# The node stage of a graph layer made in two passes: source rows first, target rows second

## The chip, the cores and the metric

One core of one Trainium2 chip runs the kernel. The metric is the device time of one execution in microseconds (us). The engines are TensorE (PE; PEld is its weight loads), VectorE (DVE), ScalarE (ACT), GpSimd (POOL) and SyncE (SP), and 16 DMA engines move data.

## The reference

The layer has N = 12500 nodes with C = 128 channels and E = 400000 edges, sorted by target. A node's row is normalised and clipped, and every edge makes a message from its source's and its target's row; attention weights over the edges of a target sum the messages up.

```python
h = jnp.maximum(_layernorm(x), 0.0)
msg_src = h @ w_src + b_src
msg_dst = h @ w_dst
message = (msg_src[src] + msg_dst[dst]) * edge_weight * radial_mlp(edge_attr)
message = message @ w_sep + b_sep            # 8 heads of 16 alpha and 16 value channels
alpha, value = smooth_leaky_relu(message[:, :, :16]), message[:, :, 16:]
score = einsum(alpha, alpha_dot)             # one number per edge and head
att = segment_softmax(score, dst)
out = segment_sum(value * att, dst) @ w_proj + b_proj
return x + out
```

The radial MLP has two hidden layers of 64 with silu, on 32 edge attributes.

## The kernel before, in words

The kernel has a node stage, an edge stage and a tail, all written with an order fixed by hand: each engine executes its instructions in the order of the program text, and semaphores, placed by the framework, make one engine wait for another.

**Node stage (lines 150 to 347, 0 to about 111 us).** The 12500 rows are 98 tiles of up to 128 rows, in 25 groups of four ("quads"). x is loaded whole into `x_all` at the start. `stats` (L214) takes mean and variance of a group of tiles on DVE (L218, L219), the square root on ACT (L221), the reciprocal and the shift on DVE (L222, L223). `norm(i)` (L231) makes h = relu(x * rstd + shift) of a quad on ACT, four instructions. `turn(i)` transposes the four tiles on PE (L240), and DVE copies the turned quad from PSUM to `hT` (L243). `products(i)` multiplies each tile by w_src and w_dst side by side, 256 columns (L255, PE), copies the result from PSUM to `ms` on ACT (L261) or for some on DVE (L259), and SP stores it to two DRAM tables, `t_src` and `t_dst` (L266, L268). The loop over the quads issues, for quad i: `stats` of two quads where i is even, `norm(i+2)`, `turn(i+1)`, `products(i)`. Besides, SP issues `load_targets` at i = 5 (all 400000 targets into `cur`, and the ends of all sections of 500 edges) and `load_weights` at i = 9 (33 small loads); at i = 15 `fits` counts on DVE whether the targets are sorted (L273 a comparison, L276 a sum) and every section spans less than 64 rows (`bad`, which chooses between this path and a slower one that these inputs don't take); at i = 20 `cuts` marks on DVE where the target changes (L305, `sm`), and makes small constants with PE and DVE (`bvb`, L313, `pv`, `pb`).

**Edge stage (`windows`, L663; about 111 to 4115 us).** It works in steps of 1000 edges, two sections of 500; `step(k)` runs for k from -5 to 399 and holds one piece each of several steps, later ones ahead of earlier ones. The pieces that matter here:

- `prep_load(u)`, `prep_make(u)`, `prep_turn(u)` (L675 to L706): for 16 steps, the source numbers of the edges are loaded by SP, turned by PE into a list `idx` for the gathers, and the targets into `loc`. For u = 0 they stand ahead of the first step, later ones inside steps.
- `load_e` (L710, issued by ACT), `load_w`, `load_md`, `load_d`, `load_sm` (issued by SP): edge attributes `e_t`, edge weights `w_b`, the 64 rows of t_dst from the section's first target on (`md`, L727, at an address read from `base`), the targets, and the marks.
- `zero(i)` (L131, SP): the output table `agg` is set to zero in 20 stores from `z`, two a step in steps 0 to 9.
- `gather(k, f)` (L749, POOL): for each 128 edges one indirect DMA brings the 128 source rows of t_src into `gs0` or `gs1`, of three buffers each. 3125 of them in all, 7.8 a step. In step k stand the gathers of step k+2.
- `e_T`, `mlp1`, `mlp2`, `mlp3`, `radial`: the radial MLP.
- `sources(k, f)` (L819, L822, PE) turns the gathered rows into PSUM; `message(k)` (L829) adds the target rows there by a product with the one-hot matrix `ohT`, and multiplies by the radial part (L835, `mT`, DVE).
- `alphas`, `scores` (L840 to L864) and, 13 steps later (`LAG`), `values` and `sums` (L926, L937).

**Tail (about 4115 to 4313 us).** Window sums are combined, and the finish stage makes the output projection (L1304, `py`) and adds x.

The functions that the change touches, with the lines of the profile:

Of the kernel before, what the change touches and what calls it, by code (L numbers as in the profile page):

```python
# [30 lines left out]
P = 128  # L31
# [25 lines left out]
def gnn_kernel(ctx: ExitStack, tc: tile.TileContext, a: dict, out: bass.AP):  # L57
# [68 lines left out]
    dst_h = dst.rearrange("(k f e) -> f k e", f=2, e=SEC)  # L126
# [22 lines left out]
    with tc.tile_pool(name="node", bufs=2) as np_, tc.tile_pool(name="node1", bufs=1) as n1, \  # L149
# [15 lines left out]
        CC = E // P  # L165
        cur = n1.tile([P, CC + 1], I32, name="cur")
# [9 lines left out]
        def load_targets():  # L176

            nc.sync.dma_start(out=cur[:, 1:CC + 1], in_=dst.rearrange("(p c) -> p c", p=P))
            at = dst[CC - 1:CC]
            with nc.allow_non_contiguous_dma(reason="single targets"):  # L180
                nc.sync.dma_start(out=cur[1:P, 0:1], in_=bass.AP(at.tensor, at.offset, [[CC, P - 1], [1, 1]]))
                for f in range(2):
                    nc.sync.dma_start(out=base[:, f, :], in_=dst_h[f:f + 1, :, 0])
                at = dst[0:1]
                nc.sync.dma_start(out=ends, in_=bass.AP(
                    at.tensor, at.offset, [[8 * SEC, 100], [SEC, 8], [SEC - 1, 2]]))

        def load_weights():
            for name, t in wt.items():
                ap = a[name]  # L190
                if name == "b_src":
                    ap = ap.rearrange("o c -> c o")
                elif name == "b_proj":
                    ap = ap.to_broadcast([P, C])
                nc.sync.dma_start(out=t, in_=ap)
            for f in range(2):
                for q in range(2):
                    o = (2 * q + f) * RAD
                    nc.sync.dma_start(out=w1b[o:o + RAD, f * FC:(f + 1) * FC], in_=a["fc_w1"])
                s = slice(f * FC, (f + 1) * FC)  # L200
                for q in range(2):
                    nc.sync.dma_start(out=w2b[s, q * FC:(q + 1) * FC], in_=a["fc_w2"])
                nc.sync.dma_start(out=w3b[s, :], in_=a["fc_w3"])
                nc.sync.dma_start(out=b12[s, 0:1], in_=a["fc_b1"])
                nc.sync.dma_start(out=b12[s, 1:2], in_=a["fc_b2"])
# [6 lines left out]
        hs, hTs = {}, {}  # L212
        G = 8
        def stats(t0, t1):  # L214
            for t in range(t0, t1):
                n = rows(t)
                st = np_.tile([P, nc.vector.BN_STATS_DIM], F32, name="st", bufs=4)
                nc.vector.bn_stats(st[:n], x_all[:n, t, :])  # L218
                nc.vector.bn_aggr(mv[:n, t, :], st[:n])  # L219
            s = slice(t0, t1)  # L220
            nc.scalar.activation(rstd[:, s], mv[:, s, 1], AF.Sqrt, bias=eps, scale=1.0)  # L221
            nc.vector.reciprocal(rstd[:, s], rstd[:, s])  # L222
            nc.vector.scalar_tensor_tensor(shift[:, s], mv[:, s, 0], -1.0, rstd[:, s],  # L223
                                           op0=ALU.mult, op1=ALU.mult)
# [21 lines left out]
        def products(i):  # L246
            t0, t1 = quads[i]
            hT = hTs.pop(i)
            ms = np_.tile([P, 2, 4, C], F32, name="ms", bufs=6)
            for v0 in range(t0, t1, 2):  # L250
                vs = range(v0, min(v0 + 2, t1))
                pm = nps.tile([P, 2, 2, C], F32, name="pm", bufs=4)
                for t in vs:
                    n = rows(t)
                    nc.tensor.matmul(pm[:n, t - v0], hT[:, t - t0, :n], w_nodes, start=True, stop=True)  # L255
                for n, u0, u1 in blocks(v0, vs[-1] + 1):
                    o, q = ms[:n, :, u0 - t0:u1 - t0, :].rearrange("p k j c -> p j k c"), pm[:n, u0 - v0:u1 - v0]
                    if v0 % 16 == 2:
                        nc.vector.tensor_copy(o, q)  # L259
                    else:  # L260
                        nc.scalar.copy(o, q)  # L261
# [41 lines left out]
        def cuts():  # L303
# [16 lines left out]
            nc.vector.tensor_scalar(b_s, pb, 0.25, None, op0=ALU.mult)  # L320
            nc.vector.tensor_sub(far, eb[:, :, 1], eb[:, :, 0])
# [339 lines left out]
    def windows():  # L661
# [5 lines left out]
        with tc.tile_pool(name="wk2", bufs=2) as sp, tc.tile_pool(name="ps", bufs=1, space=PSUM) as pp, \  # L667
                tc.manual_schedule(), ExitStack() as held:
            lp = held.enter_context(tc.tile_pool(name="ld", bufs=2))
            prep, e_g, d_g, w_g, md, gath = {}, {}, {}, {}, {}, {}  # L670
            eTs, h1s, h2s, ohT, m3, mr, mTs, als, S_all, sms, Ps, Pem, pvx, ohs, accs, xs, Ms, pms, p3s, rads = (
                {} for _ in range(20))


            def prep_load(u):  # L675
# [10 lines left out]
                prep[u] = (ri, rb)  # L686

            def prep_make(u):
                ri, rb = prep[u]
# [5 lines left out]
                prep[u] = rows  # L695

            def prep_turn(u):
                rows = prep[u]
# [3 lines left out]
                idx = lp.tile([P, T], I32, name="idx")  # L702
                nc.vector.tensor_copy(idx, pt[:, 0, 0:T])
# [660 lines left out]
```

## Time and profile before

| quantity | value |
|---|---|
| median of 3 runs (lowest, highest) | 4316.28 us (4314.72, 4322.2) |
| the profiled execution | 4315.26 us |
| its span | 4313.4 us |
| mean granted clock of TensorE | 0.977 |
| first and last gather (L749) start | 118.41 and 4107.08 us |
| DMA over the span | 790.10 MB, 183 GB/s |

The page has the busy time of each engine, the span in 40 slices, the DMA queues, the chain of work that ended last, and the costliest groups of instructions. A line of the timeline reads: start, duration, engine, line, operation, tile written and tiles read, count, and in brackets the idle time of the engine before it with what ended that. A line of the waits reads: engine, tile and line that waited, what it waited for, total us, times, longest us.

### The profile page before, as it was taken

What the parts mean: (1) busy time and instruction counts of PE and PEld (TensorE: products, weight loads), DVE (VectorE), ACT (ScalarE), POOL (GpSimd) and SP (SyncE); (2) the same over time, 40 slices, a digit from 0 to 9 for tenths busy, and PEclk for the clock granted to TensorE, in tenths of its full rate; (3) what the DMA queues carried; (4) which work ended last, traced back from release to release, by engine and by line L of the source; (5) the groups of instructions that cost most, each with busy time, mean ns of one, the idle gap of its engine ahead of it and who ended that gap; (6) DMA issues with size and microseconds to landing.
All of it is one profiled execution on the core that took longest, in us unless ns stands there. A gap on an engine that the chain in (4) does not pass through costs nothing.

```text
span 4313.4 us, 91919 instructions
## 1 busy us (share of the span) xinstructions
PE 4065.7 (94%) x31567; PEld 2626.4 (61%) x31567; DVE 3101.8 (72%) x5980; ACT 2105.5 (49%) x4995; POOL 3037.4 (70%) x3148
## 2 busy tenths in 40 slices
PE   6679999999999999999999999999999999999974
PEld 5346666666666666666666666666666666666653
DVE  7357777777777777777777777777777777777776
ACT  6335555555455455455555455454555545544521
POOL 0667777777777777777777777777777777777701
PEclk8789999999999999999999999999999999999987
DMA  5667777777777777777777777777777767777725
GB/s 207 196 183 183 183 193 184 192 194 185 194 188 186 192 190 186 192 183 185 198 186 193 185 177 190 183 182 185 175 181 188 177 182 184 182 185 178 173 59 190
DMA packets 598603, 790.10 MB, mean 183 GB/s; under 512 B 125595, under 2 KB 475424, under 8 KB 597996
## 3 DMA queue, kind: packets, MB, share of 16 engines
q1 hardware_dynamic: 394314, 520.94, 43.1%
q0 software_dynamic: 100416, 205.45, 23.2%
q10 hardware_dynamic: 103394, 57.74, 5.1%
q8 instruction: 250, 4.10, 0.4%
q14 instruction: 229, 1.88, 0.1%
HBM read 643.48 MB, written 140.67 MB: 182 GB/s over the span
## 4 chain that ended last, share of the span: by engine, by line
PE 80%; DMA 8%; ACT 3%; DVE 3%; issue 2%; POOL 2%; SPq 1%; ACTq 0%; POOLq 0%; DVEq 0%
PE V L926 16%; PE pa L840 14%; PE misc L937 9%; PE pm L829 6%; PE p L800 6%; PE pm L819 6%; PE p L783 5%; PE m L768 5%; PE m L854 4%; PE pm L822 4%; DMA gs<-t_src,idx 4%; POOL gs L749 2%; PE m L759 2%; ACT L842 1%; DMA agg<-z 1%
## 5 line engine op out<-in xcount | busy, mean ns | idle before, releaser
L749 POOL DMA_INDIRECT gs<-t_src,idx x3125 | 3023.0, 967 | 1082.9 <-issue 778.6
L842 ACT ACTIVATE sl<-pa,c_b_a 128x500 f32<-128x500 f32 x800 | 541.8, 677 | 1004.4 <-PE pa L840 996.8
L926 PEld LDWEIGHTS V<-c_w_v,mT 128*125 128x125 f32 x6192 | 735.3, 188 | 479.8 <-DVE ohT L793 231.9
L928 DVE TENSOR_TENSOR pvx<-V,Pem 125x512 f32<-125x512 f32 x774 | 530.9, 686 | 524.2 <-PE V L926 495.5
L926 PE MATMUL V<-c_w_v,mT 128*125 128x128 f32 x6192 | 875.3, 285 | 0.2 <-DVE pvx L928 0.2
L840 PE MATMUL pa<-mT,c_w_a 128*128 128x500 f32 x1600 | 817.4, 593 | 53.8 <-DVE al L847 51.8
L847 DVE SCALAR_TENSOR_TENSOR al<-pa,sl 128x500 f32<-128x500 f32 x800 | 542.3, 678 | 239.6 <-ACT sl L842 227.0
L822 PEld LDWEIGHTS pm<-ident,gs 128*128 128x128 f32 x2350 | 418.6, 192 | 380.0 <-issue 359.5
L807 DVE SCALAR_TENSOR_TENSOR rad<-p,c_fc_b,w_b 128x500 f32<-128x500 f32 x800 | 553.3, 733 | 104.2 <-PE p L800 101.4
L835 DVE SCALAR_TENSOR_TENSOR mT<-pm,c_b_src,rad 128x500 f32<-128x500 f32 x800 | 553.2, 733 | 79.9 <-PE pm L829 66.1
L937 PE MATMUL misc<-pvx,oh 125*64 125x136 f32 x6400 | 463.7, 288 | 0.0
L937 PEld LDWEIGHTS misc<-pvx,oh 125*64 125x64 f32 x6400 | 361.1, 138 | 163.7 <-ACT eT L761 157.3
L819 PE MATMUL pm<-ident,gs 128*128 128x128 f32 (+9 forms) x2725 | 436.9, 275 | 13.1 <-DMA gs<-t_src,idx 12.7
L800 PE MATMUL p<-h,w3b 64*128 64x500 f32 x1600 | 406.5, 585 | 11.1 <-ACT h L786 11.1
L786 ACT ACTIVATE h<-p,b 128x500 f32<-128x500 f32 x400 | 326.3, 816 | 177.1 <-PE p L783 134.5
L941 ACT COPY ob<-misc 128x136 f32<-128x136 f32 x400 | 108.9, 272 | 618.3 <-PE misc L937 533.7
L822 PE MATMUL pm<-ident,gs 128*128 128x12 f32 (+30 forms) x2350 | 384.2, 244 | 16.5 <-DMA gs<-t_src,idx 15.7
L819 PEld LDWEIGHTS pm<-ident,gs 128*128 128x128 f32 (+9 forms) x2725 | 339.2, 157 | 30.2 <-DMA gs<-t_src,idx 18.3
L829 PE MATMUL pm<-ohT,m 64*128 64x500 bf16 x2400 | 325.6, 378 | 0.0
L840 PEld LDWEIGHTS pa<-mT,c_w_a 128*128 128x128 f32 x1600 | 243.1, 192 | 81.4 <-DVE al L847 65.6
L768 PE MATMUL m<-eT,w1b 64*128 64x250 f32 x800 | 276.7, 426 | 7.5 <-ACT Sp L857 6.5
L768 PE MATMUL misc<-eT,w1b 64*128 64x250 f32 x800 | 276.7, 426 | 0.0
(151 smaller groups left out, 4227.0 us busy)
## 6 DMA issues: line engine op xcount, KB each, us to landing
w_b<-in_edge_weight SPq DMA_DIRECT2D x400, 500.0 KB
d_b<-in_dst SPq DMA_DIRECT2D x400, 250.0 KB
e_t<-in_edge_attr ACTq DMA_DIRECT2D x400, 125.0 KB
gs<-t_src,idx POOLq DMA_INDIRECT x3125
sc_d<-Sp SPq DMA_DIRECT2D x200, 250.0 KB
win<-ob SPq DMA_DIRECT2D x400, 68.0 KB
agg<-ob SPq DMA_DIRECT2D x800, 33.5 KB
md<-t_dst SPq DMA_DIRECT2D x800, 32.0 KB
```

The costliest lines, as they stand in the source:

```text
L749: nc.gpsimd.indirect_dma_start(out=gs[:, t - t0, :], out_offset=None, in_=t_src[:, :], in_offset=bass.IndirectOffsetOnAxis(ap=idx[:, t:t + ...
L768: nc.tensor.matmul(p1[q], w1b[s, :], eTs[k][s, :], start=True, stop=True)
L800: nc.tensor.matmul(p3s[k][:, f, 0:SEC], w3b[s, :], h2s[k][s, :], start=True, stop=True)
L807: nc.vector.scalar_tensor_tensor(rad[:, s], p3[:, f, 0:SEC], b3, w_g[k][:, s], op0=ALU.add, op1=ALU.mult)
L819: nc.tensor.matmul(pms[k, f][:, a - e0:b - e0], gath[k // 16, t][:n], ident[:n, :n], start=(a == e0), stop=False, is_transpose=True, skip_ ...
L822: nc.tensor.matmul(pms[k, f][:, a - e0:b - e0], gath[k // 16, t], ident[:, a - t * P:n], start=(a == e0), stop=False, skip_group_check=True)
L829: nc.tensor.matmul(pms[k, f], m3[k][s, j, :], ohT[k][s, :], start=False, stop=(j == 2), skip_group_check=True)
L835: nc.vector.scalar_tensor_tensor(mTs[k][:, s], pms.pop((k, f)), b_n, rad[:, s], op0=ALU.add, op1=ALU.mult)
L840: nc.tensor.matmul(pa, w_a, mTs[k][:, f * SEC:(f + 1) * SEC], start=True, stop=True)
L842: nc.scalar.activation(sl, pa, AF.Silu, bias=b_a, scale=1.0)
L926: nc.tensor.matmul(V[:, t, :], mTs[c][:, o:o + T], w_v, start=True, stop=True)
L937: nc.tensor.matmul(acc[f * W:(f + 1) * W, :], ohs[c][:, f * TS + t, :], pvx[c][:, f, t, :], start=(t == 0), stop=(t == TS - 1), skip_group ...
```

## The change

- The quads are gone through twice. Pass 1 makes only the product with w_src, 128 columns, and stores t_src; pass 2 makes the product with w_dst and stores t_dst. The turned rows stay in `x_all` between the passes. All copies out of PSUM are on ACT; t_dst is stored in groups of eight tiles.
- In pass 1 the order for quad i is `turn(i+1)`, `products(i, 0)`, `stats` of quad i+4, `norm(i+2)`, and for odd i `scales` (square root, reciprocal, shift) of two quads.
- `load_targets` stands at i = 1, without the two strided loads of `base`, which `cuts` now copies on DVE from `eb`. The 33 weight loads are issued two a quad from i = 3.
- The comparison for the order check is cut in four (`falls`, i = 8 to 11), and PE counts it by seven products with a column of ones (`fits`, i = 13). `cuts` stands behind the first quad of pass 2.
- The source list of the first 16 steps, `idx0`, is made in the node stage (`first`, i = 6). What `prep_load(0)`, `prep_make(0)` and `prep_turn(0)` still make, `loc` of the first 16 steps, is moved into steps 2, 4 and 5.
- The pool of the edge stage's loads (`ld`, which holds `gs`, `e_t`, `md` and others) is laid on the other side of the memory.

```diff
             with nc.allow_non_contiguous_dma(reason="single targets"):
                 nc.sync.dma_start(out=cur[1:P, 0:1], in_=bass.AP(at.tensor, at.offset, [[CC, P - 1], [1, 1]]))
-                for f in range(2):
-                    nc.sync.dma_start(out=base[:, f, :], in_=dst_h[f:f + 1, :, 0])
...
+        def weights_list():
...
+            return [lambda t=t, ap=ap: nc.sync.dma_start(out=t, in_=ap) for t, ap in pairs]
...
+        def scales(t0, t1):
             s = slice(t0, t1)
             nc.scalar.activation(rstd[:, s], mv[:, s, 1], AF.Sqrt, bias=eps, scale=1.0)
...
-            hTs[i] = np_.tile([P, 4, P], F32, name="hT", bufs=3)
             w = (t1 - t0 - 1) * P + rows(t1 - 1)
-            nc.vector.tensor_copy(hTs[i].rearrange("p u n -> p (u n)")[:, :w],
+            nc.vector.tensor_copy(x_all[:, t0:t1, :].rearrange("p u n -> p (u n)")[:, :w],
                                   pt.rearrange("p u n -> p (u n)")[:, :w])
-        def products(i):
+        def products(i, k):
             t0, t1 = quads[i]
-            hT = hTs.pop(i)
-            ms = np_.tile([P, 2, 4, C], F32, name="ms", bufs=6)
-            for v0 in range(t0, t1, 2):
-                vs = range(v0, min(v0 + 2, t1))
-                pm = nps.tile([P, 2, 2, C], F32, name="pm", bufs=4)
-                for t in vs:
-                    n = rows(t)
-                    nc.tensor.matmul(pm[:n, t - v0], hT[:, t - t0, :n], w_nodes, start=True, stop=True)
-                for n, u0, u1 in blocks(v0, vs[-1] + 1):
-                    o, q = ms[:n, :, u0 - t0:u1 - t0, :].rearrange("p k j c -> p j k c"), pm[:n, u0 - v0:u1 - v0]
-                    if v0 % 16 == 2:
-                        nc.vector.tensor_copy(o, q)
-                    else:
-                        nc.scalar.copy(o, q)
+            pm = nps.tile([P, 4, C], F32, name="pm", bufs=4)
+            for t in range(t0, t1):
+                n = rows(t)
+                nc.tensor.matmul(pm[:n, t - t0], x_all[:, t, :n], w_nodes[:, k, :], start=True, stop=True)
+            u = 4 * (i % 2) if k else 0
+            if u == 0:
+                mds[k] = np_.tile([P, 4 + 4 * k, C], F32, name=f"ms{k}", bufs=4 if k else 6)
+            ms = mds[k]
+            for n, u0, u1 in blocks(t0, t1):
+                o, q = ms[:n, u + u0 - t0:u + u1 - t0, :], pm[:n, u0 - t0:u1 - t0]
+                nc.scalar.copy(o, q)
+            if k and i % 2 == 0 and i + 1 < Q:
+                return
+            table = (t_src, t_dst)[k]
+            tv = table[0:NF * P, :].rearrange("(p t) c -> p t c", t=NF)
+            t0 -= u
             f1 = min(t1, NF)
-            for k, table in enumerate((t_src, t_dst)):
-                tv = table[0:NF * P, :].rearrange("(p t) c -> p t c", t=NF)
-                if t0 < f1:
-                    nc.sync.dma_start(out=tv[:, t0:f1, :], in_=ms[:, k, 0:f1 - t0, :])
-                if t1 > NF:
-                    nc.sync.dma_start(out=table[NF * P:N, :], in_=ms[:tail, k, NF - t0, :])
+            if t0 < f1:
+                nc.sync.dma_start(out=tv[:, t0:f1, :], in_=ms[:, 0:f1 - t0, :])
+            if t1 > NF:
+                nc.sync.dma_start(out=table[NF * P:N, :], in_=ms[:tail, NF - t0, :])
+        idx0 = const.tile([P, T], I32, name="idx0")
+        def first():
+            ri = n1.tile([T, P], I32, name="ri")
+            nc.sync.dma_start(out=ri, in_=src.rearrange("(t p) -> t p", p=P)[0:T, :])
+            rows_0 = n1.tile([T, P], F32, name="rows_0")
+            nc.vector.tensor_copy(rows_0, ri)
+            pt = nps.tile([P, T], F32, name="tot", bufs=1)
+            nc.tensor.transpose(pt, rows_0, ident[:T, :T])
+            nc.vector.tensor_copy(idx0, pt)
+        gt = n1.tile([P, CC], BF16, name="gt")
+        def falls(j):
+            s0, s1 = j * CC // 4, (j + 1) * CC // 4
+            nc.vector.tensor_tensor(gt[:, s0:s1], cur[:, s0:s1], cur[:, s0 + 1:s1 + 1], op=ALU.is_gt)
         def fits():
-            gt = n1.tile([P, CC], BF16, name="gt")
-            nc.vector.tensor_tensor(gt, cur[:, 0:CC], cur[:, 1:CC + 1], op=ALU.is_gt)
-            cnt = n1.tile([P, 2], F32, name="cnt")
+            cnt = n1.tile([P, 1], F32, name="cnt")
             nc.vector.memset(cnt, 0.0)
-            nc.vector.tensor_reduce(cnt[:, 0:1], gt, AX.X, ALU.add)
             span = n1.tile([100, 8], F32, name="span")
             nc.vector.tensor_sub(span, ends[:, :, 1], ends[:, :, 0])
             nc.vector.tensor_scalar(span, span, float(W - 1), None, op0=ALU.is_ge)
-            nc.vector.tensor_reduce(cnt[:100, 1:2], span, AX.X, ALU.add)
-            tot = nps.tile([1, 1], F32, name="tot", bufs=1)
-            for j in range(2):
-                nc.tensor.matmul(tot, cnt[:, j:j + 1], ones[:, 0:1], start=(j == 0), stop=(j == 1))
-            nc.vector.tensor_copy(bad, tot)
+            nc.vector.tensor_reduce(cnt[:100, :], span, AX.X, ALU.add)
+            tot = nps.tile([1, BANK], F32, name="tot", bufs=1)
+            for o in range(0, CC, BANK):
+                w = min(BANK, CC - o)
+                nc.tensor.matmul(tot[:, :w], ones_b, gt[:, o:o + w], start=(o == 0), stop=False,
+                                 skip_group_check=True)
+            nc.tensor.matmul(tot[:, 0:1], cnt, ones[:, 0:1], start=False, stop=True, skip_group_check=True)
+            sum_ = n1.tile([1, 1], F32, name="sum_")
+            nc.vector.tensor_reduce(sum_, tot, AX.X, ALU.add)
...
+            nc.vector.tensor_copy(base.rearrange("o f k -> o k f"),
+                                  eb[0:1, :, 0].rearrange("o (k f) -> o k f", f=2))
...
-        stats(0, 4)
-        norm(0)
-        stats(4, G)
-        norm(1)
+        for i in range(2):
+            stats(*quads[i])
+            scales(*quads[i])
+            norm(i)
         turn(0)
+        for i in (2, 3):
+            stats(*quads[i])
+        scales(quads[2][0], quads[3][1])
+        more = iter(weights_list())
         for i in range(Q):
-            if i % 2 == 0 and 4 * i + G < NB:
-                stats(4 * i + G, min(4 * i + 2 * G, NB))
+            if i + 1 < Q:
+                turn(i + 1)
+            products(i, 0)
+            if i + 4 < Q:
+                stats(*quads[i + 4])
             if i + 2 < Q:
                 norm(i + 2)
-            if i + 1 < Q:
-                turn(i + 1)
-            products(i)
-            if i == 5:
+            if i % 2 and i + 3 < Q:
+                scales(quads[i + 3][0], quads[min(i + 4, Q - 1)][1])
+            if i == 1:
                 load_targets()
-            if i == 9:
-                load_weights()
-            if i == 15:
+            if i == 6:
+                first()
+            if i >= 3:
+                for load in (next(more, None), next(more, None)):
+                    if load:
+                        load()
+            if 8 <= i < 12:
+                falls(i - 8)
+            if i == 13:
                 fits()
-            if i == 20:
+        for i in range(Q):
+            products(i, 1)
+            if i == 0:
                 cuts()
...
-            lp = held.enter_context(tc.tile_pool(name="ld", bufs=2))
+            lp = held.enter_context(tc.tile_pool(name="ld", bufs=2, side="right"))
...
-                idx = lp.tile([P, T], I32, name="idx")
-                nc.vector.tensor_copy(idx, pt[:, 0, 0:T])
+                if u:
+                    idx = lp.tile([P, T], I32, name="idx")
+                    nc.vector.tensor_copy(idx, pt[:, 0, 0:T])
+                else:
+                    idx = idx0
...
-            prep_load(0)
-            prep_make(0)
-            prep_turn(0)
+            prep[0] = (idx0, None)
             for k in range(2):
                 load_e(k)
...
+                if k == 2:
+                    prep_load(0)
...
+                if k == 5:
+                    prep_turn(0)
+                if k == 4:
+                    prep_make(0)
```

More of the change, by code (lines that the diff above doesn't have):

```diff
@@ L125, in gnn_kernel @@
     base = const.tile([1, 2, NP], I32, name="base")
-    dst_h = dst.rearrange("(k f e) -> f k e", f=2, e=SEC)
     def zero(i):
@@ L165, in gnn_kernel @@
         CC = E // P
+        ones_b = n1.tile([P, 1], BF16, name="ones_b")
+        nc.vector.memset(ones_b, 1.0)
         cur = n1.tile([P, CC + 1], I32, name="cur")
@@ L186, in load_targets @@
                     at.tensor, at.offset, [[8 * SEC, 100], [SEC, 8], [SEC - 1, 2]]))
-        def load_weights():
+        def weights_list():
+            pairs = []
             for name, t in wt.items():
@@ L194, in load_weights @@
                     ap = ap.to_broadcast([P, C])
-                nc.sync.dma_start(out=t, in_=ap)
+                pairs.append((t, ap))
             for f in range(2):
@@ L198, in load_weights @@
                     o = (2 * q + f) * RAD
-                    nc.sync.dma_start(out=w1b[o:o + RAD, f * FC:(f + 1) * FC], in_=a["fc_w1"])
+                    pairs.append((w1b[o:o + RAD, f * FC:(f + 1) * FC], a["fc_w1"]))
                 s = slice(f * FC, (f + 1) * FC)
                 for q in range(2):
[L202 to L205, printed above, removed]
+                    pairs.append((w2b[s, q * FC:(q + 1) * FC], a["fc_w2"]))
+                pairs += [(w3b[s, :], a["fc_w3"]), (b12[s, 0:1], a["fc_b1"]), (b12[s, 1:2], a["fc_b2"])]
+            return [lambda t=t, ap=ap: nc.sync.dma_start(out=t, in_=ap) for t, ap in pairs]
         mv = n1.tile([P, NB, 2], F32, name="mv")
@@ L211, in gnn_kernel @@
         shift = n1.tile([P, NB], F32, name="shift")
-        hs, hTs = {}, {}
+        hs, mds = {}, {}
         G = 8
@@ L279, in fits @@
             nc.vector.tensor_scalar(span, span, float(W - 1), None, op0=ALU.is_ge)
[L280 to L284 removed]
+            nc.vector.tensor_reduce(cnt[:100, :], span, AX.X, ALU.add)
[7 more added lines that the diff above has]
+            nc.vector.tensor_reduce(sum_, tot, AX.X, ALU.add)
+            nc.vector.tensor_copy(bad, sum_)
             nc.sync.dma_start(out=ends_d[:, 1:2 * NS + 1].rearrange("o (p c) -> (o p) c", p=100),
@@ L668, in windows @@
                 tc.manual_schedule(), ExitStack() as held:
-            lp = held.enter_context(tc.tile_pool(name="ld", bufs=2))
+            lp = held.enter_context(tc.tile_pool(name="ld", bufs=2, side="right"))
             prep, e_g, d_g, w_g, md, gath = {}, {}, {}, {}, {}, {}
-            eTs, h1s, h2s, ohT, m3, mr, mTs, als, S_all, sms, Ps, Pem, pvx, ohs, accs, xs, Ms, pms, p3s, rads = (
-                {} for _ in range(20))
+            eTs, h1s, h2s, ohT, m3, mr, mTs, als, S_all, sms, Ps, Pem, pvx, ohs, accs, xs, Ms, pms, p3s, rads, made = (
+                {} for _ in range(21))
             def prep_load(u):
@@ L685, in prep_load @@
                     nc.sync.dma_start(out=rb, in_=at)
-                prep[u] = (ri, rb)
+                made[u] = (ri, rb)
             def prep_make(u):
-                ri, rb = prep[u]
+                ri, rb = made[u]
                 rows = lp.tile([P, 2, P], F32, name="rows", bufs=1)
@@ L694, in prep_make @@
                 nc.vector.tensor_scalar(rows[:, 1, 0:T], ri[:, 1, 0:T], rf, None, op0=ALU.subtract)
-                prep[u] = rows
+                made[u] = rows
             def prep_turn(u):
-                rows = prep[u]
+                rows = made.pop(u)
                 pt = pp.tile([P, 2, P], F32, name="misc")
```

## The prediction

> **What bounds the kernel now.** The page comes first. It names TensorE (PE) on 94% of the span and on 80% of the chain that ended last, while GpSimd (POOL) is busy for 70%:
>
> ```profile
> PE 4065.7 (94%) x31567; PEld 2626.4 (61%) x31567; DVE 3101.8 (72%) x5980; ACT 2105.5 (49%) x4995; POOL 3037.4 (70%) x3148
> PE 80%; DMA 8%; ACT 3%; DVE 3%; issue 2%; POOL 2%; SPq 1%; ACTq 0%; POOLq 0%; DVEq 0%
> ```
>
> A busy share doesn't show a queue that never waits, so the timeline and the waits of POOL come second. Its 3125 gathers of source rows (L749) last 967 ns each; what follows them is:
>
> ```profile
> 118.41 1.12 POOL L749 DMA_INDIRECT gs<-t_src,idx  x1 [116.22 <-DVE loc L705]
> ...
> 254.88 0.94 POOL L749 DMA_INDIRECT gs<-t_src,idx  x1 [0.30 <-issue]
> 267.26 0.94 POOL L749 DMA_INDIRECT gs<-t_src,idx  x1 [11.44 <-PE pm L822]
> 268.50 0.94 POOL L749 DMA_INDIRECT gs<-t_src,idx  x1 [0.30 <-issue]
> ...
> 4107.08 0.94 POOL L749 DMA_INDIRECT gs<-t_src,idx  x1 [0.30 <-issue]
> ```
>
> ```profile
> POOL gs L749 <- issue: 778.6, 2553, 0.6
> POOL gs L749 <- DVE loc L705: 116.2, 1, 116.2
> POOL gs L749 <- PE pm L822: 36.7, 78, 11.4
> ```
>
> Nearly every gap is the 0.3 us between two issues, so the pitch is 0.97 + 0.30 = 1.27 us, 7.8 gathers or 9.95 us for a step of 1000 edges. From the first gather (118.4) to the last (4108.0) POOL stands still only once for long, 11.4 us before 267.26 (with two short halts 14 us); it then waited for `sources(11)`, which frees the third buffer of `gs`. After that nothing on PE, DVE or ACT delays it. So the time is: the moment at which the fill releases the gather at 267.26, then the rest at 1.27 us each, then 205 us of tail (4108 to 4313). A change of the node stage counts only as far as it moves that release.
>
> Third, the chain between 118 and 267 tells what sets it. Gathers up to 155, then:
>
> ```profile
> 165.26 13.16 DMA e_t<-in_edge_attr
> ...
> 211.50 14.01 DMA agg<-z
> ...
> 236.87 12.70 DMA w_b<-in_edge_weight
> 249.66 9.45 DMA sc_d<-Sp
> ```
>
> The fill is a stream of SP and ACT transfers that land after 9 to 14 us each, with PE between them. The stretches of the windows view (PE, PEld, DVE, ACT, POOL busy; granted clock; DMA share; GB/s):
>
> ```profile
> 14.60:24.80 10.20, 8.13 (x37) 5.63 (x37) 6.81 (x26) 7.84 (x20) 0.00 (x0) 1.00 0.63 247
> 24.80:28.20 3.40, 3.40 (x12) 2.76 (x11) 2.91 (x17) 2.63 (x7) 0.00 (x0) 0.50 0.42 158
> ...
> 112.00:262.00 150.00, 100.34 (x517) 48.95 (x517) 56.39 (x110) 46.73 (x103) 104.20 (x110) 0.79 0.67 196
> ```
>
> PE is busy for 100 of the fill's 150 us.
>
> **Pass 1.** Before, a pair of quads takes 6.8 us (the square roots on ACT stand at 14.48, 21.22, 28.03), 3.4 a quad for both tables. After, DVE would need 2.5: four statistics pairs of 0.395, a turned copy 0.69, half of reciprocal and shift 0.19. But the order of issue makes a ring. ACT holds copy(i), then norm(i+2); PE holds turn(i+1), then products(i). So norm(k) is followed by turn(k), products(k-1), copy(k-1) and only then norm(k+1): no two of them overlap. Before, norm(i+2) stood ahead of copy(i) and no such ring closed. Its terms, from these rows, are
>
> ```profile
> 15.25 1.65 ACT L231 ACTIVATE h<-x_all,shift,rstd 128x128 f32<-128x128 f32 x4 [0.47 <-DVE shift L223]
> 16.80 0.56 ACT L261 COPY ms<-pm 128x512 f32<-128x512 f32 x1
> ...
> 4249.35 1.06 PE L1304 MATMUL py<-c_w_proj,qT 128*128 128x128 f32 x8
> ```
>
> norm 1.65; the last transpose behind it 0.3; the products at the finish stage's matmul of the same shape, of which 0.9 lie on the path; the copy 0.56; half a square root 0.15: 3.5 to 3.6 us a quad. The halved products save nothing, as ACT stands while PE works. The prologue is unchanged: norm(2) ends at 16.95, so norm(23) ends at 16.95 + 21 x 3.54 = 91.3, and copies 22 to 24 follow until about 96.5. `first()` stands on PE ahead of turn(8), behind a cast that waits for its landing: about 2.5 (0 to 4). `fits()` puts seven matmuls behind a count on DVE: 2.4 (0 to 4). Half clock: seven windows of 3.4 us in the old stage, in which these matmuls took 1.92 for 1.06 (4258.45); I take four, each 1.4 dearer (0.86 for the products, some 0.5 for transposes, an estimate), 5.6 in all (0 to 10). Pass 1 ends at about 107, the first gather stands one issue and one landing (0.5 + 3.6) later, at 111 instead of 118.4.
>
> A rule of the Trainium skill speaks against that last term: "TensorE: Matmul & The Clock Gate", section "HAM oscillation — how this bites in real kernels", lets the clock fall only for idle gaps of PE above some 3.4 us, which the ring has not; by it the 5.6 would go. The trace does not agree: 24.80 to 28.20 runs at 0.50, and PE had not been idle for over 1.43 us in the ten us before.
>
> **Pass 2.** Products(0) 0.95. `cuts()` then puts two products behind DVE's 3.41 (sm) + 0.98 + 0.28 + 0.09 + 0.17 + 0.22 = 5.2 us, of which 3.7 are not covered (0 if DVE starts them early); 1.1 for them; 24 quads of 0.95, 22.8; half clock after that stall 1.7. PE ends near 136, the last store of t_dst is issued near 137. The first load of md came 4.6 us after it (110.33, 114.96): now at 141, 26 later. e_T(0), 117.52 before, has its input behind ACT's last copy: 141, 23.5 later.
>
> **Fill.** Gathers 1 to 24 (steps 0 to 2, 30 us) run from 111 to 141 beside pass 2; then POOL waits for `sources(0)`, the end of pass 2 coming first. So the 7 us of earlier start buy nothing by themselves: POOL stands at 24 gathers at 148.4 in the old run as well. What they buy is that PE finds the rows there: its waits for gathers in the fill are 8.9 us (3.79, 1.61, 0.83, 2.03, 0.44 and less), and all lie ahead of 165 on the chain. Behind 165 the transfers' waits stay. `prep_load(0)`, three issues of 0.29 + 0.43 + 0.64 in SP's queue at step 2, with 0.65 on DVE and 0.9 on PE at steps 4 and 5, cost about 1 (0 to 2). Against that SP and POOL lose them ahead of the fill, counted in the 141.
>
> **Rest.** Four comparisons of 0.85 (falls) lie in DVE's slack of 1 us a quad; if it were gone, 3.4. The 33 weight loads, two a quad at 0.43 to 0.6, lie in SP's 3.5. The copy of `base` on DVE (about 0.9, in pass 2) replaces two strided loads; the md loads wait for the later t_dst anyway. The gathers in pass 2 share DMA with 6.4 MB of t_dst: at 247 GB/s (14.60:24.80) 26 us, so stores can end as late as PE does, 0 to 4 more. Tail and pitch are not touched.
>
> **Sum.** Against the profiled run's own 4315.3 (span 4313.4 and 1.9 around it; the median of the runs is 1.0 above): md and e_T +24.5, gather waits -8.9, prep +1: the release at 267.26 moves by +16.6, and everything after it as well. 4332 on the profile, 4333 on the median.
>
> **Rivals.**
> - Faster. The fill no longer waits for landings: fewer gathers compete there, and sources(1) to (11) follow at POOL's 9.95 us. For: mT(0) to mT(5) ended at 136.9 to 186.4, 9.9 a step with 4.9 of gather waits in it. Against: 5 to 11 took 14.1 a step, with the chain on e_t, agg and w_b, which all stay. Then POOL restarts at 150 instead of 148.4 and the 14 us of halts go: 4303 to 4305. It decides if the 132 us from sources(0) to sources(11) become under 110.
> - No change: the ring doesn't hold ACT, and pass 1 runs at DVE's 2.6 a quad: 20 us less, 4313. Any pitch below 2.9 leads there. Against: issue order is fixed on each engine.
> - Much slower: the fill's length is set by transfers from its first step, and the gather waits only hid landings of e_t and agg: +24.5 and up to 4 of stores, 4340 to 4345.
> - Full clock: if the ring's short gaps bring no half clock, 5.6 in pass 1 and 1.7 in pass 2 go: 4326. For: the core ran at 1.00 from 41.80 to 69.20 with like gaps. Against: 24.80 to 28.20, above. This is what the rule named there would give.
>
> **Numbers.** Forecast 0.46; faster 0.16; no change 0.14; much slower 0.20; full clock 0.04. A measurement tells 0.2%, 8.6 us, from no change. The forecast's own spread (4322 to 4340) puts 0.03 more into no change. So faster 0.16, within 0.17, slower 0.67. The range reaches up through the slower case and down past no change to the edge of the faster case, most of which (0.14) it leaves out: 4305 to 4346; the forecast's own is 4322 to 4340.
>
> **What would show it.** Right: norms, products and copies of pass 1 one behind another at 3.5 us; first gather near 111; POOL idle after its 24th for about 10 us; PE idle 3.7 in `cuts()`; first md near 141; the third buffer's long wait near 283; pitch 1.27 and tail 205 as before. Wrong: a pitch below 3, a fill without POOL's long wait, or a last gather before 4108.

## The result, and the profile after

The changed kernel takes 4344.59 us (median of 4 runs, 4338.95 to 4346.87), the kernel before 4315.65 us in the same set. The ratio, taken from the means, is 1.0062, 95% interval 1.0044 to 1.0079: slower by 27 us (29 between the medians). The profiled execution took 4346.87 us (span 4345.1), 31.6 more than that of before. On the page, the busy shares of the engines are those of before within 1%, and the chain is almost the same:

```profile
PE 79%; DMA 9%; ACT 3%; DVE 3%; POOL 3%; issue 2%; SPq 1%; ACTq 0%; POOLq 0%; DVEq 0%
```

The timeline of POOL and its waits tell more (start, duration, idle time before it and what ended that):

```profile
121.19 1.43 POOL L790 DMA_INDIRECT gs<-t_src,idx  x1 [119.01 <-DMA same<-sm]
...
163.22 0.94 POOL L790 DMA_INDIRECT gs<-t_src,idx  x1 [11.62 <-PE pm L863]
...
299.04 0.94 POOL L790 DMA_INDIRECT gs<-t_src,idx  x1 [13.77 <-PE pm L863]
...
4139.18 0.94 POOL L790 DMA_INDIRECT gs<-t_src,idx  x1 [0.30 <-issue]
```

```profile
POOL gs L790 <- issue: 779.2, 2555, 0.6
POOL gs L790 <- PE pm L863: 52.7, 75, 13.8
```

The first gather starts 2.8 us later than before (118.41), not earlier. The 25th waits 11.6 us for `sources(0)`. The release that stood at 267.26 stands at 299.04, 31.8 later. Behind it nothing differs: from gather 250 to gather 3125 it is 3660.3 us before and 3660.2 after, and from the last gather to the end of the span 206.3 and 205.9.

The 31.8 us in two parts: e_T(0), the first PE work of the edge stage, starts at 151.28 instead of 117.52, 33.8 later; from there to the release it takes 147.8 us instead of 149.7, 2.0 less. The node stage lost 34 us, and the fill gave 2 back.

**Pass 1.** One turn of its loop, in the timeline of the changed kernel:

```profile
24.13 1.65 ACT L233 ACTIVATE h<-x_all,shift,rstd 128x128 f32<-128x128 f32 x4
24.68 1.63 PE L242 MATMUL pt<-ident,h 128*128 128x128 f32 x4 [1.07 <-ACT h L233]
26.10 1.92 PE L253 MATMUL pm<-w_nodes,x_all 128*128 128x128 f32 x8
28.05 0.59 ACT L260 COPY ms<-pm 128x512 f32<-128x512 f32 x1 [2.27 <-PE pm L253]
28.54 1.65 ACT L233 ACTIVATE h<-x_all,shift,rstd 128x128 f32<-128x128 f32 x4
```

The transposes follow the norm tile by tile; the products start where the transposes end, the copy where the products end, and the next norm behind the copy. ACT stands 2.27 us while PE makes the products, PE stands 1.07 us while ACT makes the norm: the ring of the prediction. A turn takes 28.54 - 24.13 = 4.41 us here, as the products last 1.92 us; where they last 1.06 us a turn takes 3.44 (norms at 36.38 and 39.82).

Two moments of PE and a stretch of the windows view (PE, PEld, DVE, ACT, POOL busy; granted clock; DMA share; GB/s) show when each holds:

```profile
38.25 1.06 PE L253 MATMUL pm<-w_nodes,x_all 128*128 128x128 f32 x8
43.70 0.47 PE L281 MATMUL tot<-ident,rows 125*128 125x125 f32 x1 [4.40 <-DVE rows L279]
```

```profile
90.00:118.00 28.00, 21.60 (x84) 16.60 (x83) 12.63 (x42) 13.18 (x33) 0.00 (x0) 0.50 0.15 56
```

By the starts of the norms, 17 of the 22 turns that follow one another take 4.40 us, three take 3.44, and the two with the waits of `first()` and `fits()` take 7.4 and 6.2. The longer pitch is the ring at half clock: wherever this trace has a record of the clock, the products last 1.9 us at 0.50 and 1.06 us at full. The records begin at 32.40; ahead of that the windows view prints 1.00 for want of one, but the products last 1.92 there, in the first four turns of the ring too. At 43.70 PE had waited 4.40 us for the source numbers of `first()`, and the clock is at half from 42.64 to 73.36. The Trainium skill, "TensorE: Matmul & The Clock Gate", section "HAM oscillation — how this bites in real kernels", lets the clock fall where PE idles for more than about 3.4 us; at this place the trace agrees. The clock falls twice more, at 76.78 behind `fits()` and from 87.02 to 117.74. Ahead of the last fall PE had not been idle for more than 1.07 us at a time since 76.60.

**Pass 2** went as forecast: the products of 24 quads take 22.7 us (121.45 to 144.17; forecast 22.8), the wait in `cuts` 2.0 (forecast 3.7).

**The fill.** The waits of PE, the first line from before (115 to 290), the second from after (148 to 310):

```profile
PE pm L819 <- DMA gs<-t_src,idx: 8.9, 6, 3.8
```

```profile
PE p L824 <- DVE rad L848: 24.0, 4, 8.7
```

The waits for gathered rows are gone, and waits for the radial part stand in their place (3.8 us before). DVE makes the radial part right behind the one-hot matrix `ohT`, which needs the loaded targets `d_b`. Ahead of each of the four waits of PE (6.1, 4.0, 8.7 and 5.2 us) DVE had waited for a landing of `d_b` (7.6, 5.4, 10.1 and 6.7 us). The third pair:

```profile
241.83 0.48 DVE L834 TENSOR_SCALAR ohT<-d_b,tgt 128x500 bf16<-128x500 int32 x1 [10.12 <-DMA d_b<-in_dst]
```

```profile
243.66 1.11 PE L824 MATMUL p<-h,w2b 64*64 64x250 f32 x8 [8.68 <-DVE rad L848]
```

The chain of the changed kernel goes from landing to landing:

```profile
191.95 11.13 DMA rb<-in_dst
...
213.54 10.70 DMA ri<-in_src
...
231.89 9.91 DMA d_b<-in_dst
...
254.31 12.34 DMA agg<-z
267.06 14.44 DMA w_b<-in_edge_weight
281.58 9.45 DMA sc_d<-Sp
```

`rb` belongs to `prep_load(0)`, which the change moved into the fill; `ri` belongs to the `prep_load` of the next 16 steps, which both kernels have there. No run takes the moved loads alone out of the changed kernel, so what they cost there is open; in e4, the kernel before with them and with `first()`, the stretch from e_T(0) to the release takes 150.9 us instead of 149.7.

### The profile page after: what moved, and what is told of

Same layout as the page of the kernel before. It is cut to its first block, busy times and chain, and to the rows that moved or that the text cites. A ratio compares the mean times of both kernels' runs of the same rounds, so it can differ in the third digit from the quotient of the medians.

```text
span 4345.1 us, 92340 instructions
## 1 busy us (share of the span) xinstructions
PE 4087.5 (94%) x31769; PEld 2646.9 (61%) x31769; DVE 3094.2 (71%) x5980; ACT 2113.2 (49%) x5003; POOL 3038.9 (70%) x3148
## 4 chain that ended last, share of the span: by engine, by line
PE 79%; DMA 9%; ACT 3%; DVE 3%; POOL 3%; issue 2%; SPq 1%; ACTq 0%; POOLq 0%; DVEq 0%
PE V L967 16%; PE pa L881 13%; PE misc L978 9%; PE p L841 6%; PE pm L870 6%; PE pm L860 6%; PE p L824 5%; PE m L809 4%; PE m L895 4%; PE pm L863 4%; DMA gs<-t_src,idx 4%; POOL gs L790 2%; PE m L800 2%; PE pm L253 1%; DMA max_d<-M 1%
## 5 line engine op out<-in xcount | busy, mean ns | idle before, releaser
L978 PE MATMUL misc<-pvx,oh 125*64 125x136 f32 x6400 | 462.1, 287 | 0.0
L824 PE MATMUL p<-h,w2b 64*64 64x250 f32 x3200 | 265.0, 402 | 24.0 <-DVE rad L848 24.0
```

The costliest lines, as they stand in the source:

```text
L978: nc.tensor.matmul(acc[f * W:(f + 1) * W, :], ohs[c][:, f * TS + t, :], pvx[c][:, f, t, :], start=(t == 0), stop=(t == TS - 1), skip_group ...
```

## The experiments

The chips differ by some 10 us for one kernel (before: 4315.65, 4307.67, 4305.97), and the pitch of the gathers differs a little between executions. So a ratio is always to the kernel before on the same chip, and the times in the expectations, which count from the 4316 us of the first chip, are held against these ratios. Places are compared by the start of gather 250 in the profiled run; from it to the last gather it is 3648 to 3661 us in all kernels of the table. The column "fill" is the time from e_T(0) to the 111th gather, the one that stood at 267.26:

| kernel | e_T(0) | gather 1 | fill | gather 250 | ratio to before, 95% interval |
|---|---|---|---|---|---|
| before | 117.5 | 118.4 | 149.7 | 446.7 | 1 |
| changed | 151.3 | 121.2 | 147.8 | 479.0 | 1.0062 (1.0044 to 1.0079) |
| e1, norm ahead of the copy | 118.7 | 88.0 | 145.5 | 443.6 | 0.9994 (0.9983 to 1.0004) |
| e2, ri loaded early | 138.1 | 107.9 | 148.1 | 465.6 | 1.0056 (1.0041 to 1.0070) |
| e3, agg set to zero in pass 1 | 146.5 | 124.6 | 125.1 | 447.0 | 1.0032 (1.0020 to 1.0044) |
| e4, before with idx0 | 123.8 | 126.0 | 150.9 | 453.6 | 1.0019 (1.0010 to 1.0027) |
| f1, one pass, norm ahead | 106.0 | 106.9 | 151.1 | 436.0 | 0.9977 (0.9968 to 0.9986) |
| f2, f1 with e2's and e3's edits | 146.7 | 146.7 | 138.7 | 462.1 | 1.0051 (1.0038 to 1.0065) |
| f3, e1 with e2's and e3's edits | 144.3 | 121.2 | 125.1 | 445.5 | 1.0014 (1.0005 to 1.0023) |
| f4, before with e3's edit | 170.8 | 171.7 | 139.6 | 487.3 | 1.0095 (1.0079 to 1.0110) |

**e1: the ring undone.**

```diff
         for i in range(Q):
+            if i + 2 < Q:
+                norm(i + 2)
             if i + 1 < Q:
                 turn(i + 1)
             products(i, 0)
...
-            if i + 2 < Q:
-                norm(i + 2)
```

> The changed kernel with norm(i+2) issued at the head of pass 1's loop, ahead of the copy of products(i, 0), as the kernel before had it; nothing else is changed. In the changed kernel a quad of pass 1 takes 4.40 us (norms at 92.06, 96.46, 100.86). Theory of the ring (norm, turn, products, copy, norm, each behind the other): without it ACT needs 1.65 + 0.59 + 0.15 = 2.4 us a quad, DVE 2.5 and PE at half clock 1.63 + 1.72 = 3.4, so a quad takes 2.6 to 3.4, pass 1 ends 20 to 35 us earlier, and the time falls by as much: 4310 to 4325. Rival, the half clock alone is at fault and the order of issue costs nothing: a quad stays above 4 us and the time within 8 us of the changed kernel's.

The ratio falls from 1.0062 to 0.9994, 29 us. The timelines of ACT and of POOL in e1:

```profile
20.49 1.65 ACT L233 ACTIVATE h<-x_all,shift,rstd 128x128 f32<-128x128 f32 x4 [0.53 <-DVE shift L225]
25.72 1.65 ACT L233 ACTIVATE h<-x_all,shift,rstd 128x128 f32<-128x128 f32 x4 [0.53 <-DVE shift L225]
```

```profile
87.99 1.12 POOL L790 DMA_INDIRECT gs<-t_src,idx  x1 [85.80 <-DVE sm L328]
...
131.04 0.94 POOL L790 DMA_INDIRECT gs<-t_src,idx  x1 [11.80 <-PE pm L863]
...
264.10 0.94 POOL L790 DMA_INDIRECT gs<-t_src,idx  x1 [13.38 <-PE pm L863]
```

Two quads take 25.72 - 20.49 = 5.2 us, 2.6 a quad, and what ends ACT's wait is DVE. Five of the ten pairs take 5.2 to 5.4; with the slower ones, among them those with `first()` and `fits()`, it is 3.1 a quad. Gather 1 starts 33 us earlier than in the changed kernel, gather 250 35 us. So the order of two steps on ACT accounts for the whole loss, half clock included, and the rival is refuted. But POOL starts 30 us ahead of the kernel before and ends 3 us ahead of it: it stands 11.8 us behind its 24th gather, until pass 2 and the first loads are through, and some 27 us more in the fill, where before it stands 13 (gathers 25 to 250 take 312.5 us in e1, 298.0 before, and 285.0 in f2, which has no halt).

**e2: the gap in front of `first()`.**

```diff
-            nc.sync.dma_start(out=ri, in_=src.rearrange("(t p) -> t p", p=P)[0:T, :])
...
+            if i == 0:
+                nc.sync.dma_start(out=ri_0, in_=src.rearrange("(t p) -> t p", p=P)[0:T, :])
```

> The changed kernel with the load of the first source numbers (ri) issued at quad 0 instead of quad 6; its cast and its transpose stay at quad 6. In the changed kernel PE waits 4.40 us for them before 43.70, and from there to 118 the clock is near 0.5 although it was 1.00 from 14 to 41 with the same work. Theory of the gap: that wait of more than one 3.41 us window drops the clock, and the ring at half clock is not busy enough to raise it again. Without the gap the clock stays at 1.00 and a quad at 3.5 until the next gap, at the worst the one at quad 13: 9 to 20 us less, 4325 to 4336. Rival, the clock falls in the ring by itself: only the wait of 2.5 us goes, 4340 to 4343.

In the profiled run PE's wait for `ri` is 0.8 us instead of 4.40. But the products ran at half speed from the first turn on, ahead of `first()` (42.18) and for two turns behind it. Full speed begins behind those, with no long wait of PE ahead of it. Two products of one loop, 4.3 us apart:

```profile
48.28 1.91 PE L253 MATMUL pm<-w_nodes,x_all 128*128 128x128 f32 x8
...
52.58 1.06 PE L253 MATMUL pm<-w_nodes,x_all 128*128 128x128 f32 x8
```

Gather 250 comes 13.4 us earlier than in the changed kernel. The ratio, 1.0056, is not apart from 1.0062 by the intervals, and the six runs spread over 15 us (4321.41 to 4336.59). Neither theory holds as it stands: the ring was at half clock with no long wait ahead of it, and it also came out of it by itself. What the gap is worth stays open.

**e3: the zero stores moved into pass 1.**

```diff
-                if 0 <= 2 * k < NZ:
-                    for i in range(2 * k, min(2 * k + 2, NZ)):
-                        zero(i)
...
+            if 3 <= i < 3 + NZ:
+                zero(i - 3)
```

> The changed kernel with the 20 stores that set agg to zero issued one a quad in pass 1, from quad 3 on, instead of two a step in steps 0 to 9. In the changed kernel the fill, from e_T(0) at 151.3 to the release of POOL at 299.0, takes 147.7 us, and 149.7 in the kernel before, although the gathers were there 20 us ahead. Theory of the landings: the fill's length is set by transfers that land after 9 to 14 us; without these 20 stores (6.8 MB) the chain loses its pieces agg<-z and the fill shortens by 10 to 30 us: 4315 to 4335. Rival, the fill is set by something else (the first scores and their store at its end): within 5 us, 4340 to 4349, and POOL's wait near 299 stays.

In the profiled run the halt near 299 is gone: behind gather 25 POOL waits only once for more than 1 us (2.45 us at 166.9). The ratio falls by 0.0030, 13 us; gather 250 comes 32 us earlier, but that run was the fastest of its six (4309.75, median 4318.52), and 5 of the 32 us lie ahead of e_T(0). So these stores held the fill, and the rival is refuted. Whether it is their landings, their bytes or their places in SP's queue isn't separated: the edit takes all three out of the fill.

**e4: idx0 alone, in the kernel before.**

```diff
+            if i == 6:
+                first()
...
-            prep_load(0)
-            prep_make(0)
-            prep_turn(0)
+            prep[0] = (idx0, None)
```

> The kernel before with one part of the change: the first 16 steps' source list is made in the node stage at quad 6 (first, idx0), and prep_load(0), prep_make(0) and prep_turn(0) stand in steps 2, 4 and 5. One pass, one table order, all else as before. The first gather then needs only t_src: about 113.5 instead of 118.4. Theory of the prediction: PE's waits for gathers in the fill (8.9 us) shrink by 5, the release at 267 comes 4 to 6 us earlier: 4309 to 4312. Rival, what the changed kernel shows: the landings take the room back, and e_T(0) comes 2 us earlier at most: 4312 to 4317.

It is slower, 1.0019, and both theories missed: the 4315.23 us fall into the rival's range only because this chip is faster, where before takes 4307.67. Two lines of its timeline:

```profile
47.33 0.23 DVE L277 CAST rows<-ri 125x128 f32<-125x128 int32 x1 [11.40 <-DMA ri<-in_src]
47.61 0.47 PE L279 MATMUL tot<-ident,rows 125*128 125x125 f32 x1 [13.07 <-DVE rows L277]
```

The source numbers are issued at 44.23, behind the other loads in SP's queue; DVE waits 11.4 us for them, PE 13.1. The next reciprocals stand at 34.92 and 53.21, 18.3 us apart where 6.8 is usual, and the node stage ends 11 us later (last store of t_dst issued at 121.38 instead of 110.33). Saving the list ahead of the fill brought less than waiting for it in the node loop cost.

**A chip on which nothing could be compared.** Four kernels ran on a chip that took 35% longer for all of them, the kernel before too (5798.44 us), with gaps on every engine; the bound there is not POOL's pitch, so the times say nothing on the fill. The ratios were: the changed kernel again (e5) 1.0058 (1.0027 to 1.0089), f1's kernel (e6) 0.9982 (0.9951 to 1.0012), f4's (e7) 1.0110 (1.0068 to 1.0153), f3's (e8) 1.0054 (1.0021 to 1.0088).

> The changed kernel itself, once more, on the chip of the runs below, since the kernel before differs by 8 us between the chips of the first two sets (4315.65 and 4307.67). What is asked: does a quad of pass 1 take 4.40 us in every run, or 4.40 in some and 3.44 in others, as the trace with the early load of ri shows within one run (4.40 up to 50.71, 3.44 behind it)? If the order of issue alone sets the pitch, every run has 4.4 and the ratio to before is again 1.006. If the ring leaves TensorE at the edge between half and full clock, the runs spread by up to 24 x 0.96 = 23 us and the ratio lies between 1.002 and 1.007.

The node stage of e5 still answers its question: norms start 3.44 us apart from 15.39 to 36.04, PE then waits 4.34 us for `ri`, and from 43.41 to 69.81 they start 4.40 apart. The same ring has two pitches in one run, and the long wait lies between them. Later, at 90.65, it falls from 3.44 back to 4.4 with no such wait ahead of it.

> The changed kernel with the second pass folded into the first (products(i, 0) and products(i, 1) one behind the other in one loop), norm(i+2) at the head of the loop, and cuts at quad 20, as the kernel before has it; all other parts of the change stay. Against e1_norm_ahead it differs in the two passes alone. There the first gather was at 88.0 but the first md and e_T(0) at 118.2 and 118.7, and POOL stood for 11.8 us behind its 24th gather. Theory that the second pass costs more than the early gathers bring: with one pass a quad takes about 3.0 us (ACT 1.65 + 1.18 + 0.15, PE 0.9 + 2.1), the first gather comes near 105, md and e_T(0) at 105 to 112, 6 to 13 us earlier than in e1, and the time falls below e1's by that: ratio to before 0.996 to 0.998. Theory that the early gathers pay: e6 is slower than e1 by 3 us or more, ratio 1.000 to 1.002.

> The kernel before with the 20 stores that set agg to zero issued one a quad in the node stage (quads 3 to 22) instead of two a step in steps 0 to 9; nothing of the change. In the changed kernel this took POOL's wait near 299 away (e3_zero_early). Theory of the landings: in the kernel before they make the halts of 11.4, 1.2 and 2.0 us as well, so the time falls by 10 to 14 us (ratio 0.9968 to 0.9977), unless the node stage gets longer by them. Rival, the halt at 267 comes from the store of the first scores and the loads behind it: ratio 0.999 to 1.001.

> The changed kernel with three edits together: norm(i+2) at the head of pass 1's loop (e1), the load of ri at quad 0 (e2), and the zero stores in pass 1 (e3). In e1 POOL stood for 11.8 us behind its 24th gather and for 25 us in the rest of the fill. If the zero stores make the 25 us, as in e3, POOL never waits behind sources(0), and the time is e1's less 24 and less 2 to 5 for ri: ratio to before 0.992 to 0.994, faster than both kernels. If the stores crowd the shorter pass 1 (now some 3 us a quad) and delay t_src, part of it comes back: 0.995 to 0.998.

The last three were run again on another chip, as f1, f4 and f3.

**f1: one pass, the rest of the change kept.**

```diff
             products(i, 0)
+            products(i, 1)
...
+            if i == 20:
+                cuts()
-        for i in range(Q):
-            products(i, 1)
-            if i == 0:
-                cuts()
```

> The kernel of e6_one_pass once more, as the chip of that set ran every kernel 35% longer and told nothing of the fill: the changed kernel with both products of a quad in one loop, norm(i+2) at its head, cuts at quad 20. Against e1_norm_ahead only the second pass is undone. There gather 1 started at 88.0, e_T(0) at 118.7, gather 250 at 443.6. If the second pass costs more than its early gathers bring: gather 1 near 100 to 106, e_T(0) before 112, gather 250 at 430 to 438, ratio to before 0.996 to 0.998. If the early gathers pay: gather 250 behind 446, ratio 1.000 or above.

As the first theory said, with gather 1 some 1 us behind its range: 0.9977, the fastest of all, and faster than both kernels (4294.96 us, before 4305.97 on that chip). POOL in f1:

```profile
257.07 0.94 POOL L789 DMA_INDIRECT gs<-t_src,idx  x1 [12.29 <-PE pm L862]
```

Its first gather is 19 us behind that of e1, yet gather 250 is 7.6 us ahead, because e_T(0) is 12.7 us ahead and there is no halt behind the 24th gather. Two passes bring POOL work that it can't go on from: the fill takes 145 to 151 us in the six kernels that have the zero stores in it, whether the gathers start 30 us ahead of e_T(0) (changed, e1, e2) or within 2 us of it (before, e4, f1).

**f2, f3, f4: the zero stores in shorter node loops.**

> f1_one_pass with the load of ri at quad 0 and the 20 zero stores of agg in the loop from quad 3 on. If the landings of the zero stores make POOL's halts in the fill (25 us in e1, 7 in e3), POOL runs nearly without a halt from its first gather: that start plus 3125 x 1.272 plus 205, so with a start near 100 about 4285 on a chip where before takes 4310: ratio 0.993 to 0.995. If the stores lengthen the node loop instead (they share the DMA engines with the loads of x and the stores of both tables), 0.996 to 0.999.

> The kernel of e8_two_pass_best once more on another chip: the changed kernel with norm(i+2) at the head of pass 1's loop, the load of ri at quad 0, and the zero stores in pass 1. Gather 1 near 86 to 92, POOL's halt behind its 24th gather stays at about 10 us (sources(0) waits for pass 2), the later 25 us of halts go: gather 250 at 418 to 428, ratio 0.993 to 0.996. Against f2_one_pass_all this tells whether two passes pay once the ring and the stores are out of the way: POOL's start plus its one halt, 88 + 10, against f2's start near 100, so within 5 us of each other.

> The kernel of e7_before_zero once more on another chip: the kernel before with the 20 zero stores in the node stage (quads 3 to 22). If they make the halts of 11.4, 1.2 and 2.0 us behind gather 108, gather 250 starts at 432 to 437 instead of 446.7 and the ratio is 0.9968 to 0.998. If the node loop grows by them as much, 0.999 to 1.001.

All three times missed. The halts do go: in f2 and f4 no wait of POOL behind its first gather is longer than 0.3 us up to gather 250, and the gaps between the gathers of f2 read

```profile
POOL gs L793 <- issue: 771.7, 2532, 0.3
```

The fill falls to 139 us in f2 and f4, which is the pitch of 111 gathers, and to 125 in e3 and f3, whose gathers start 22 to 23 us ahead of it: with the stores out of the fill the early gathers do pay there. But the node stage grows by more than the halts were worth: gather 1 moves to 146.7 (106.9 in f1), 121.2 (88.0 in e1) and 171.7 (118.4 before). One issue of a table store before, and one in f4:

```profile
108.33 0.42 SPq L266 DMA_DIRECT2D t_dst<-ms  x1
```

```profile
98.82 3.13 SPq L266 DMA_DIRECT2D t_dst<-ms  x1
```

SP issues in order, and its issues themselves get longer. Ahead of the first gather the 52 issues of table stores take 56.4 us in f4 instead of 25.4, and the issues of the zero stores 23.3: 54 us, where gather 1 moves by 53. In f2 the same two terms are 19.5 and 22.1 us, against 40 (f1 to f2). These are sums; not every issue need lie on the chain. The table stores leave late, and ACT waits 25.5 us in f4 for the buffers of `ms` that they free (not at all before). Now and then SP also waits until an earlier zero store has landed; in the chain of f4 stand

```profile
65.26 9.98 DMA agg<-z
...
124.35 10.21 DMA agg<-z
```

In e3 this cost little, likely because a quad took 3.4 to 4.4 us anyway. So the 20 stores have to be paid somewhere, and neither place tried is free.

## Why the prediction was right or wrong

- **The bound.** Right: pitch, tail and everything behind the release are the same in both traces, and the whole difference lies ahead of gather 112.
- **The ring in pass 1.** Right, and e1 shows that it is the cause: without it the loss is gone. The turn was put at 3.54 us and takes 3.44 at full clock. DVE's pace without the ring was given as 2.5 to 2.6 a quad; e1 has it in half of its pairs.
- **The half clock in it.** The first mis-sized term. The sum took four turns at half clock, each 1.4 dearer, 5.6 us. In the trace 17 turns ran at it, each 0.96 dearer, 16 us. Six of them stand behind the wait of `first()`, four ahead of it from the start of the ring, one behind `fits()`, and six behind a fall with no long wait. So the step that failed is the count, taken from the old loop, where the ring didn't close; why the ring stays so long at half clock is not shown. The turn with `first()` was 4.0 dearer, too, not 2.5. md and e_T(0) were put 24.5 later; e_T(0) came 33.8 later. That is 9 of the 15 us by which the release, put at 283.9 (267.26 + 16.6), missed 299.04.
- **The fill.** The second mis-sized term: "gather waits -8.9, prep +1". The waits went, but 2.0 us were gained, as waits behind other landings took their room. The prediction had read the chain rightly, gathers up to 155 and landings behind, but added up waits as if the landings were not due at the same time. The other 6 us of the error.
- **Luck.** The stated range held 4344.59 because it reached up to the case called much slower (4340 to 4345, chance 0.20), while 4333 was put forward. That case was right on the fill, whose length the early gathers hardly changed. But it kept +24.5 for the node stage; with that and the 2.0 gained the profile would stand near 4338. That its figure met the measured one is partly luck.
- **Pass 2, cuts, DVE's and SP's small parts.** Pass 2 and `cuts` are right within 2 us each. DVE's slack, SP's small parts and prep's +1 are not told apart by any run.
- **The rivals.** The faster one (no more landings) and the unchanged one (DVE's pace) did not happen in the changed kernel; e3 and e1 show each of the two in turn. The full clock did not happen either: 17 turns ran at half, most of them without a wait above 3.4 us ahead of them.

## What to carry to other kernels

Before splitting a loop into passes, follow one item round the engines in the order of issue: a copy that stands ahead of the next item's first step on one engine makes a ring, and then halving one engine's work brings nothing (here one moved step was worth 29 us). Starting the bounding engine earlier pays only if the work that frees its buffers starts earlier too; look for the wait behind its last free buffer. A wait removed in a stretch that is full of transfers goes to the next transfer that is due, so price it by the chain without it, not by its length.

## What the runs showed of the hardware that was not expected

The ring has two steady pitches, 3.44 and 4.40 us a quad, and stays at either for up to eight turns with the same instructions (both in e2). They go with full and half clock: the same products last 1.06 and 1.91 us. What makes it change is not settled. In two runs it fell across a wait of PE of 4.3 to 4.4 us (the changed kernel, e5); but it also fell with no such wait (the changed kernel at 87.02, e3 at 53.51, e5 at 90.02), and in e2 it rose at 50.41 with none. The first record of full clock in a trace stands at 14.3 to 21.8 us in the ten runs without the ring; with it it stands at 32.40 in the changed kernel, 14.93 in the same kernel in e5, and 50.41 and 50.10 in e2 and e3. Ahead of a trace's first record the windows view prints a granted clock of 1.00, in the changed kernel from 14 to 32 while the products last 1.92; there the duration of a known instruction is the reading to go by. An issue of SP can last 1 to 3 us instead of 0.4 when many stores are under way (f4). And a store of 0.34 MB (20 of them for agg's 6.8 MB) lands only 11 to 14 us after its issue in the fill and about 10 us after it in the node stage, and what SP waits for holds up all that stands behind it.
